# Where q is projected, rotated and multiplied by sin in a one-core attention and mixture-of-experts layer

## The chip, the cores and the metric

The kernel runs on one core of one Trainium2 chip. The metric is device microseconds of one execution. Three executions of the kernel before took 1820.54, 1824.64 and 1824.67 us; their median is 1824.64 us. A further execution was recorded by the hardware profiler, and everything said of engines and waits comes from that one.

A core has five engines, each with its own instruction stream that it works through in order, held together by semaphores. The profile's names for them are PE (TensorE: matrix products, with PEld its weight loads), DVE (VectorE), ACT (ScalarE), POOL (GpSimd) and SP (SyncE, which here only issues DMAs).

## The reference

The layer is causal attention with rotary position codes (16 heads of 64, four sequences of 1024 tokens, width 256), a residual and layer norm, then a mixture of experts (top 3 of 16) with another residual and layer norm. The part that matters here is the head of the attention:

```python
def _rope(x, sin, cos):
    d = x.shape[-1] // 2
    x_hi, x_lo = (x[..., :d], x[..., d:])
    y_lo = x_lo * cos + x_hi * sin
    y_hi = x_hi * cos - x_lo * sin
    return jnp.concatenate([y_lo, y_hi], axis=-1)
proj = x @ W_in.T + b_in
...
q = _rope(q, sin, cos)
k = _rope(k, sin, cos)
att = jnp.einsum('bhqd,bhkd->bhqk', q, k) * jnp.asarray(scale, x.dtype)
att = jnp.where(mask[None, None], att, jnp.asarray(-jnp.inf, x.dtype))
att = jax.nn.softmax(att, axis=-1)
y = jnp.einsum('bhqk,bhkd->bhqd', att, v)
```

All arithmetic is in float32. The kernel keeps q and k transposed, so that the rotation is `q*sin' + swap(q)*cos`, where `swap` exchanges the 32-row halves of each head.

## The kernel before

**Pairs and slots.** The heads are worked through in pairs: 4 sequences times 8 pairs make 32 pairs n = 0 to 31. Each pair has six slots k = 0 to 5, one for each entry of `chunks = [(7,), (6,), (5,), (4,), (3, 2), (1, 0)]`, which are blocks of 128 queries; block 7 has the longest row (1024 keys), block 0 the shortest. The later half of q (queries 512 to 1023, called q1 below) is used in slots 0 to 3, the earlier half (q0) in slots 4 and 5.

**What one slot does.** `scores` (L299) multiplies q by k on PE into four PSUM buffers; DVE passes over each (L307), which adds the mask, copies to `p` and finds the row minimum `nmax`; ACT takes the exponential (L322) with a row sum; DVE inverts the sum (`rinv`, L336); POOL multiplies `p` by it (`divide`, L339); two slots later DVE transposes `p` (`turn`, L356), and PE multiplies it with v (`product`, L377). Beside that, each pair writes a part of the output projection (`out`, L399, summed into `acc` by DVE, L457), computes v for later pairs (`values`, L253, to a DRAM tile `v_d` and back by `spread` as `vr`), and prepares q and k of the next pair.

**Preparing q and k.** `project(n, i, g)` does the matrix product of x with `wqk[n]` (L215, a PSUM tile `pp`); ACT adds the bias and writes `rawq` or `rawk` (L220); DVE multiplies the same `pp` by sin into `rotq` or `rotk` (L221); SP issues four DMAs (L233) that swap the halves into `swq` or `swk`. `rotate` then multiplies the swapped copy by cos (L239) and adds it (L244), on POOL. In the instruction stream the sin product on DVE waits for a count of ACT's that includes the bias instruction on the same `pp`. While pair n runs, the next pair's k is projected in slots 0 and 1 and rotated in slot 2; q1 is projected in slot 2 and rotated in slot 4; q0 is projected in slot 5 and rotated in slot 0 of its own pair.

**PSUM.** The scores, `pp`, `oo` (of `out`) and `vv` (of `values`) all take their tiles in turn from one pool of four buffers (tag `s`). A tile that is the fourth after another takes that one's buffer, and PE waits until its readers are done.

**What sets the order.** PE runs the order of the program text, by `tc.manual_schedule`. The other engines are ordered by a scheduler from the program order and from the edges that `after` adds: in the kernel before, the sin product of every pair but the first is set behind `order["inverse"]`, the slot's `rinv`, and so behind the slot's transposes. POOL's rotations are set behind `order["divide"]`. SP issues its DMAs in the order in which the program makes them, each when what it waits for is there; `wqk` of pair n+2 is loaded by `load_qk` in slot 5 of pair n, and first used by the projection of k in slot 0 of pair n+1.

**The router.** Behind the pairs of each of the first three sequences, `router.batch` picks experts for its tokens: transposes and small DVE operations in pairs 9 to 11 (and 17 to 19, 25 to 27), then 24 `scatter` calls (L681), each an indirect DMA that POOL issues, which write table entries in pairs 12 to 14 (20 to 22, 28 to 30): four each in slots 1 and 3. `residual` (L177) adds the output bias on POOL, in slots 0 and 4 of the last pair of a sequence and near the start. After the last pair the mixture of experts runs, in lines that the change does not touch.

Of the kernel before, what the change touches and what calls it, by code (L numbers as in the profile page):

```python
# [88 lines left out]
def attention(  # L89
# [5 lines left out]
    with ExitStack() as ctx:  # L95
# [41 lines left out]
        def load_v(n):  # L137
            wv[n] = wp.tile([P, DC, 2 * P], FP, tag="wv", name="wv")
            return nc.sync.dma_start(out=wv[n], in_=w_v[n % NP // 2])

        def load_o(n):
            wo[n] = wop.tile([P, D], FP, tag="wo", name="wo")
            return nc.sync.dma_start(out=wo[n], in_=w_outT[ts(n % NP, P)])
# [24 lines left out]
        def load_router():  # L168
            router.start(late)
            for d in (x_b, *sums):  # L170
                late(nc.sync.dma_start(
                    out=d[NT:].rearrange("(p h) d -> p (h d)", p=P), in_=zero
                ))
# [21 lines left out]
        rot = {}  # L195
        raws, swps = {}, {}

        def project(n, i, g):


            b, p = divmod(n, NP)
            if i == 0:
                half = rot[n, 0, g] = qkp.tile([P, 512], FP, tag=f"rotq{g}", name="rotq")
                part = raw = qkp.tile([P, 512], FP, tag="rawq", name="rawq")
                whole = True
            else:
                whole = (n, 1) in rot
                if not whole:
                    rot[n, 1] = qkp.tile([P, T], FP, tag="rotk", name="rotk")
                    raws[n] = qkp.tile([P, T], FP, tag="rawk", name="rawk", bufs=1)  # L210
                half, raw = rot[n, 1][:, ts(g, 512)], raws[n]
                part = raw[:, ts(g, 512)]
            ps = ps_s.tile([P, 512], FP, tag="s", name="pp")
            for c in range(DC):
                nc.tensor.matmul(  # L215
                    ps, lhsT=wqk[n][:, c, i, :], rhs=xts[b, g][:, c, :],
                    start=(c == 0), stop=(c == DC - 1),
                )
            bias = bqk[:, i, p : p + 1]
            nc.scalar.activation(part, ps, AF.Identity, bias=bias)  # L220
            m = nc.vector.scalar_tensor_tensor(  # L221
                half, ps, bias, sin[:, ts(g, 512)], ALU.add, ALU.mult
            )
            if n:
                after(m, "inverse")
            if whole:

                if i == 0:
                    swp = swps[n, 0, g] = qkp.tile([P, 512], FP, tag="swq", name="swq")
                else:  # L230
                    swp = swps[n, 1] = qkp.tile([P, T], FP, tag="swk", name="swk", bufs=1)
                for r in range(4):
                    nc.sync.dma_start(out=swp[ts(r, 32), :], in_=raw[ts(r ^ 1, 32), :])  # L233
# [93 lines left out]
        order = {}  # L327

        def after(i, kind):
            tc.add_manual_dep(i.ins, order[kind].ins.name, NO_SYNC, reason="issue order")  # L330
            return i
# [53 lines left out]
        def close(n):  # L385
            p = n % NP
            yT = yp.tile([P, TC, 4, 32], FP, tag="yT")
            for a, y in enumerate(st.pop(n)):

                nc.scalar.activation(  # L390
                    yT[:, :, a, :], y[:, : 2 * P].rearrange("p (i q) -> p i q", q=32),
                    AF.Identity, bias=bv[:, p : p + 1],
                )
            st[n] = yT.rearrange("p i a q -> p (i a q)")
# [25 lines left out]
        plan = {}  # L420
        first = []

        def one_of(n):
            return 0 <= n < n_pairs

        with tc.manual_schedule(engines={mybir.EngineType.PE}):
            for n in range(n_pairs + 2):
                b, p = divmod(n, NP)
                if n == 2:
                    load_router()  # L430
                for k in range(n_slots):
                    here, before = one_of(n), one_of(n - 1)
                    part, ends = None, []
                    if k == 2 and before:
                        product(n - 1, 1)
                    if here:
                        ends = scores(n, chunks[k])
                    if k < 3 and before:
                        product(n - 1, (4, 2, 0)[k])
                        if k == 2:  # L440
                            close(n - 1)
                    if k >= 3 and here:
                        product(n, 10 - k)
                    if k in (0, 3, 4, 5) and one_of(n - 1 - (k == 0)):
                        part = out(n - 1 - (k == 0), (k - 3) % 4 if k else 3)

                    m, kk = divmod(n * n_slots + k - 2, n_slots)
                    rows = [(qc, h) for h in (1, 0) for qc in chunks[kk] if qc >= 4 * h]
                    last = "scores"
                    for i, (qc, h) in enumerate(rows):  # L450
                        if one_of(m):
                            for hh in range(2):
                                turn(m, qc, hh, h, last)
                                last = "turn"
                        if i == 0 and part:
                            a, ps = part
                            order["sum"] = after(nc.vector.tensor_tensor(a, ps, a, ALU.add), last)  # L457
                            last = "sum"
                    divide(n, ends, last)

                    if k == 0 and one_of(n + 2) and n % 2 == 0:
                        late(load_v(n + 2))
                    if k == 1 and one_of(n):
                        late(load_o(n))
                        spread(n, 1)
                    if k == 4 and one_of(n):
                        spread(n, 0)
                    if k == 5 and one_of(n + 2):
                        late(load_qk(n + 2))

                    if one_of(n + 1):
                        if k in (0, 1, 2, 5):
                            project(n + 1, int(k < 2), int(k in (1, 2)))
                        if k == 2:
                            rotate(n + 1, 1)
                        elif k == 4:
                            rotate(n + 1, 0, 1)
                    if k == 0 and one_of(n):
                        rotate(n, 0, 0)
                    if k == 0 and before:  # L480
                        product(n - 1, 3)
                    m = n + 2 - n % 2
                    if k in (3, 4) and one_of(m):
                        values(m, 2 * (n % 2) + k - 3)
                    if k in (1, 2) and n == 0:
                        values(0, k - 1)
                    if k in (0, 4):
                        if n < 2 and k == 4 * (1 - n):
                            residual(0, n)
                        if p == NP - 1 and b + 1 < B:  # L490
                            residual(b + 1, k // 4)
                    for go in plan.pop((n, k), []):
                        go()
                    if k == 1 and p == 1 and 0 < b < B:
                        normalise(b - 1, sp)
                        steps, place, scatters = router.batch(
                            b - 1, accs[b - 1], ps_s, "s", ps_s, "s"
                        )
                        for i, go in enumerate(steps):
                            plan[n + i // 2, (3, 5, 1, 3)[i]] = [go]  # L500
                        plan[n + 2, 3] = [place]
                        for i in range(6):
                            plan[n + 3 + i // 2, 1 + i % 2 * 2] = scatters[4 * i : 4 * i + 4]
                        if b == B - 1:
                            plan[n + 6, 1] = [lambda: first.extend(router.first_list())]
                            plan[n + 6, 3] = [
                                lambda: first[1](router.on_dve), lambda: first[2](ps_s, "s")
                            ]
                if b + 1 < B:
                    if p == 3:  # L510
                        load_acc(b + 1)
                    if p == 4:
                        late(load_x(b + 1, 0))
                    if p == 6:
                        late(load_x(b + 1, 1))
            assert not plan
# [597 lines left out]
```

## Time and profile before

| | |
|---|---|
| runs, median of three | 1824.64 us |
| the profiled execution: its time | 1823.27 us |
| its span (first to last instruction) | 1821.4 us |
| pairs 0 to 31: first score product to the start of pair 31's | 21.9 to 1291.2 us |
| PE busy, share of the span | 1623.9 us, 89% |
| DVE busy | 1174.7 us, 64% |
| POOL busy | 1096.9 us, 60% |
| ACT busy | 707.4 us, 39% |

The profile is read as follows. In the list of waits a row names who waited, for whom, and the total in us, the times and the longest. In a timeline each row has a start and a length in us, the engine, the line, the operation, what it writes and reads, how many were merged, and in brackets the idle time of the engine before it and what ended it. A row "SPq" is a DMA being issued, not its transfer. The granted clock of PE is a share of full speed: it was 0.95 over the whole execution, and it is either 1.00 or 0.50 in a short stretch.

### The profile page before, as it was taken

The numbers are of one execution on the slowest core, as the hardware profiler recorded it, in microseconds if no ns is written. First come the engines' busy times: TensorE is split into PE (matmuls) and PEld (weight loads), VectorE is DVE, ScalarE is ACT, GpSimd is POOL, SyncE is SP. The second block draws the span as 40 slices with busy tenths as digits, with TensorE's granted clock in tenths as the row PEclk, the third lists the DMA queues.
The fourth block names the chain that finished last, engine by engine and source line by source line (L and its number), as shares of the span: only waits on it lengthen the run. The fifth ranks groups of instructions, "written<-read, shape, count | busy, mean of one in ns | idle before, by whom it ended". The sixth has DMA issues, their size and how long they took to land.

```text
span 1821.4 us, 51884 instructions
## 1 busy us (share of the span) xinstructions
PE 1623.9 (89%) x20920; PEld 1116.8 (61%) x20920; DVE 1174.7 (64%) x3520; ACT 707.4 (39%) x1634; POOL 1096.9 (60%) x1046
## 2 busy tenths in 40 slices
PE   7899999989889998988999998899789999999980
PEld 4555555556555555655555555555468888888870
DVE  5677787787877768788777888777755222222224
ACT  3444444444444434534444443344322222222223
POOL 3655556544476754546775544477666678888542
PEclk9899999899899989999999998899999999999995
DMA  6465544474355445534454463344567989999847
GB/s 181 102 159 137 128 109 106 104 202 109 87 137 125 111 102 142 150 87 125 114 122 120 118 189 89 87 105 102 145 218 181 212 230 245 248 245 241 214 91 277
DMA packets 118167, 272.96 MB, mean 150 GB/s; under 512 B 21874, under 2 KB 72434, under 8 KB 102563
## 3 DMA queue, kind: packets, MB, share of 16 engines
q1 hardware_dynamic: 93122, 239.91, 47.7%
q0 software_dynamic: 24656, 29.68, 9.0%
q8 instruction: 167, 2.74, 0.7%
q14 instruction: 78, 0.63, 0.1%
q10 hardware_dynamic: 144, 0.01, 0.0%
HBM read 183.17 MB, written 52.79 MB: 130 GB/s over the span
## 4 chain that ended last, share of the span: by engine, by line
PE 59%; POOL 10%; DVE 9%; DMA 8%; ACT 7%; issue 6%; SPq 2%; ACTq 0%; POOLq 0%; DVEq 0%
PE s L299 11%; PE ps L882 11%; PE ps L898 10%; PE y_ps L377 10%; PE pp L215 6%; PE oo L399 4%; PE vv L253 4%; DMA wqk<-in_w_qk_dram 4%; POOL p L339 3%; ACT p L322 3%; ACT yT L390 2%; DVE p L307 2%; POOL rotq L244 1%; DMA swk<-rawk 1%; POOL swq L239 1%
## 5 line engine op out<-in xcount | busy, mean ns | idle before, releaser
L339 POOL TENSOR_SCALAR p<-p,rinv 128x512 f32<-128x512 f32 (+7 forms) x512 | 374.3, 746 | 514.9 <-DVE rinv L336 500.0
L322 ACT ACTIVATE p<-p,nmax 128x512 f32<-128x512 f32 (+7 forms) x512 | 391.8, 766 | 563.6 <-DVE nmax L307 543.6
L299 PE MATMUL s<-rotk,rotq 64*128 64x512 f32 (+3 forms) x1536 | 342.5, 539 | 107.6 <-POOL rotq L244 69.0
L299 PEld LDWEIGHTS s<-rotk,rotq 64*128 64x128 f32 x1536 | 155.2, 193 | 280.4 <-POOL rotq L244 96.5
L356 DVE STREAM_TRANSPOSE t_first<-p 128x512 f32<-128x512 f32 (+3 forms) x512 | 275.6, 581 | 0.6 <-POOL p L339 0.5
L215 PE MATMUL pp<-xT,wqk 128*128 128x512 f32 x512 | 251.8, 616 | 20.6 <-DVE nmax L307 10.2
L307 DVE CUSTOM_DVE_ANT_0 p<-s,zero 128x512 f32<-128x512 f32 x256 | 166.3, 687 | 111.8 <-PE s L299 111.6
L377 PE MATMUL y_ps<-t_first,vr 32*64 32x160 f32 (+1 forms) x8192 | 218.7, 343 | 4.5 <-DVE t_first L356 2.7
L912 POOL DMA_INDIRECT sums<-y,ids x112 | 178.9, 1598 | 69.0 <-DVE y L908 40.0
L887 ACT ACTIVATE hid<-ps,w 128x256 f32<-128x256 f32 x224 | 94.1, 471 | 314.5 <-issue 252.1
L903 DVE TENSOR_TENSOR y<-ps,w 128x512 f32<-128x512 f32 x56 | 38.7, 692 | 274.7 <-PE ps L898 274.7
L377 PEld LDWEIGHTS y_ps<-t_first,vr 32*64 32x64 f32 x8192 | 162.5, 132 | 86.0 <-DVE t_first L356 35.2
L882 PE MATMUL ps<-xg,w 128*128 128x256 f32 x896 | 204.5, 382 | 3.6 <-DVE xg L872 3.6
L898 PE MATMUL ps<-w,hid 128*128 128x256 f32 x896 | 202.6, 379 | 0.0
L898 PEld LDWEIGHTS ps<-w,hid 128*128 128x128 f32 x896 | 169.8, 190 | 23.0
L882 PEld LDWEIGHTS ps<-xg,w 128*128 128x128 f32 x896 | 167.1, 191 | 24.7 <-DVE xg L872 3.9
L215 PEld LDWEIGHTS pp<-xT,wqk 128*128 128x128 f32 x512 | 92.3, 192 | 115.2 <-issue 66.4
L399 PE MATMUL oo<-wo,yT 128*128 128x256 f32 x512 | 154.8, 428 | 1.9 <-ACT yT L390 1.7
L377 PEld LDWEIGHTS y_ps<-t_last,vr 32*64 32x64 f32 x7424 | 116.5, 137 | 63.3 <-issue 51.1
L377 PE MATMUL y_ps<-t_last,vr 32*64 32x96 f32 (+3 forms) x7424 | 141.9, 259 | 2.8 <-issue 0.8
L253 PE MATMUL vv<-wv,xT 128*128 128x256 f32 x512 | 136.4, 415 | 0.0
L307 DVE CUSTOM_DVE_ANT_0 p<-s,mask,nmax 128x512 f32<-128x512 f32 (+3 forms) x256 | 130.6, 547 | 4.4 <-PE s L299 3.9
(148 smaller groups left out, 1896.1 us busy)
## 6 DMA issues: line engine op xcount, KB each, us to landing
vr<-v_d SPq DMA_DIRECT2D x256, 256.0 KB
w<-in_wall_dram SPq DMA_DIRECT2D x56, 1154.0 KB
swk<-rawk SPq DMA_DIRECT2D x128, 128.0 KB
swq<-rawq SPq DMA_DIRECT2D x256, 64.0 KB
v_d<-v SPq DMA_DIRECT2D x128, 128.0 KB
wqk<-in_w_qk_dram SPq DMA_DIRECT2D x32, 256.0 KB
xT<-in_xT_dram SPq DMA_DIRECT2D x8, 512.0 KB
wv<-in_w_v_dram SPq DMA_DIRECT2D x16, 256.0 KB
```

The source lines that it names most:

```text
L215: nc.tensor.matmul(ps, lhsT=wqk[n][:, c, i, :], rhs=xts[b, g][:, c, :], start=(c == 0), stop=(c == DC - 1),)
L253: nc.tensor.matmul(ps[:, u, :], lhsT=xts[b, cc // 2][:, c, ts(cc % 2 * 2 + u, P)], rhs=wv[n][:, c, :], start=(c == 0), stop=(c == DC - 1),)
L299: nc.tensor.matmul(s[:, :n_k], lhsT=rot[n, 0, qc // 4][ts(hh, KD), ts(qc % 4, P)], rhs=k[ts(hh, KD), ds(k0, n_k)], start=True, stop=True,)
L307: i = nc.vector.tensor_tensor_reduce(out=probs[n, qc, hh][:, ds(k0, n_k)], in0=s[:, :n_k], in1=mask[:, 512 - n_k :] if last else zero[:, : ...
L322: nc.scalar.activation(pr, pr, AF.Exp, bias=m, scale=-1.0, accum_out=rsum[:, hh : hh + 1])
L339: order["divide"] = router.behind = nc.gpsimd.tensor_scalar(pr, pr, rinv[:, hh : hh + 1], 1.0, ALU.mult, ALU.mult)
L356: order["turn"] = router.on_dve = after(nc.vector.transpose(turned[n][h][:, hh, :, ds(i - 4 * h, n_j, step=7 - 4 * h), :], probs[n, i, hh] ...
L377: nc.tensor.matmul(st[n][a][ts(hh, KD), ds(32 * j, 32 * (TC - j))], lhsT=vrs[n, h][ts(a, 32), jh // 2 * 8 + 2 * u + jh % 2, ts(hh, KD)], r ...
L399: nc.tensor.matmul(ps[:, v, :], lhsT=st[n][:, ts(2 * h + v, P)], rhs=wo[n], start=True, stop=True,)
L882: nc.tensor.matmul(ps[:, f - f0, :], lhsT=w[:, ds(c * FF + f * P, P)], rhs=xg[:, c, :], start=(c == 0), stop=(c == DC - 1),)
L898: nc.tensor.matmul(ps[:, h, :], lhsT=hid[:, f, ts(h, P)], rhs=w[:, ds(W2_AT + f * D, D)], start=(f == 0), stop=(f == FC - 1),)
L912: s = behind(nc.gpsimd.indirect_dma_start(out=sums[t % 2], out_offset=bass.IndirectOffsetOnAxis(ap=ids[:, h, i : i + 1], axis=0), in_=y[:, ...
```

## The change

The projections of q move within slots 2 and 5 from the slot's end to just behind `scores`, ahead of the products (and of `out`). The sin product of q is set behind the slot's last score pass (`order["scores"]`) instead of behind `rinv`, and the slot's first transpose is set behind it (`order["part"]`). The projections of k stay where they were. The rotation of q1 moves from slot 4 to slot 3. Table entries, four in each of slots 1 and 3, become two in slot 0, two in slot 1 and four in slot 5.

```diff
-        def project(n, i, g):
+        def project(n, i, g, kind=None):
...
-            if n:
-                after(m, "inverse")
+            if kind:
+                after(m, kind)
+                order["part"] = m
...
-                    here, before = one_of(n), one_of(n - 1)
-                    part, ends = None, []
+                    here, before, ahead = (one_of(n + i) for i in (0, -1, 1))
+                    part, ends, last = None, [], "scores"
...
                     if here:
                         ends = scores(n, chunks[k])
+
+                    if k in (2, 5) and ahead:
+                        project(n + 1, 0, int(k == 2), last)
+                        last = "part"
                     if k < 3 and before:
                         product(n - 1, (4, 2, 0)[k])
...
-                    last = "scores"
                     for i, (qc, h) in enumerate(rows):
...
-                    if one_of(n + 1):
-                        if k in (0, 1, 2, 5):
-                            project(n + 1, int(k < 2), int(k in (1, 2)))
-                        if k == 2:
+                    if ahead:
+                        if k < 2:
+                            project(n + 1, 1, k, "inverse")
+                        elif k == 2:
                             rotate(n + 1, 1)
-                        elif k == 4:
+                        elif k == 3:
                             rotate(n + 1, 0, 1)
...
-                        for i in range(6):
-                            plan[n + 3 + i // 2, 1 + i % 2 * 2] = scatters[4 * i : 4 * i + 4]
+                        for i in range(3):
+                            for slot, c0, c1 in ((0, 0, 2), (1, 2, 4), (5, 4, 8)):
+                                plan[n + 3 + i, slot] = scatters[8 * i + c0 : 8 * i + c1]
```

In the built instruction streams, slot 2 on PE is then: scores, `pp`, product (before: scores, product, `pp`). Slot 5 is: scores, `pp`, product, `oo` (before: scores, product, `oo`, `pp`). On DVE the sin product of q stands between the last score pass and the first transpose of slots 2 and 5. On ACT `rawq` stands in slot 2 ahead of the four `yT` copies (L390), where it stood behind them; in both slots it stays behind the slot's exponentials. On POOL the pair of q1's rotation stands behind the `divide` of block 4 instead of behind those of blocks 3 and 2. On SP the four `swq` DMAs of slot 5 stand ahead of the load of `wqk`, where they stood behind it. The counts of instructions stay the same on every engine.

## The prediction

> **What bounds the kernel now.** First the busy times, then the list of waits: PE is busy 89% of the span, and its idle time is what a new order can win.
>
> ```profile
> PE 1623.9 (89%) x20920; PEld 1116.8 (61%) x20920; DVE 1174.7 (64%) x3520; ACT 707.4 (39%) x1634; POOL 1096.9 (60%) x1046
> ...
> PE s L299 <- POOL rotq L244: 69.0, 28, 6.3
> PE s L299 <- DVE rotq L221: 31.8, 30, 1.1
> PE pp L215 <- DMA wqk<-in_w_qk_dram: 9.5, 8, 5.1
> ```
>
> The first of the waits is q1's rotation, which the first scores of a pair wait for (28 of 32 pairs); the second is the sin product, which holds the PSUM buffer of the fourth score tile of slot 3; the third is k's first projection of a pair (slot 0), which waits for its weights. The change attacks the first two, at most 101 us. Next the timelines of PE and SP in pair 6, a plain one (slots begin at 249.15, 256.92, 263.73, 269.04, 275.38 and 280.78 us; pair 7 at 286.52).
>
> ```profile
> 244.06 1.07 SPq L263 DMA_DIRECT2D v_d<-v  x2
> 245.17 0.48 SPq L135 DMA_DIRECT2D wqk<-in_w_qk_dram  x1
> 248.98 2.46 SPq L233 DMA_DIRECT2D swq<-rawq  x4
> 249.15 1.99 PE L299 MATMUL s<-rotk,rotq 64*128 64x512 f32 x8 [0.95 <-POOL rotq L244]
> 253.74 1.95 PE L215 MATMUL pp<-xT,wqk 128*128 128x512 f32 x4 [0.41 <-DMA wqk<-in_w_qk_dram]
> ...
> 266.69 0.94 ACT L322 ACTIVATE p<-p,nmax 128x768 f32<-128x768 f32 x1 [3.87 <-DVE nmax L307]
> ...
> 268.15 1.26 DVE L356 STREAM_TRANSPOSE t_first<-p 128x512 f32<-128x512 f32 x2
> 270.70 0.75 DVE L221 SCALAR_TENSOR_TENSOR rotq<-pp,bqk,sin 128x512 f32<-128x512 f32 x1 [1.25 <-ACT rawq L220]
> 271.51 0.49 PE L299 MATMUL s<-rotk,rotq 64*128 64x128 f32 x2 [1.12 <-DVE rotq L221]
> ```
>
> The reader is to see two things. The sin product starts when ACT's `rawq` is done (L220: 269.98 + 0.69), so it is ACT that times it. And `wqk`, issued at 245.17, is waited for until 253.74: 8.6 us for 256 KB.
>
> **Slots 2 and 3.** The sin product now stands ahead of the transposes and still waits for `rawq`, which waits behind two exponentials. In slot 2 of pair 6: exponentials 266.69 to 268.55, `rawq` to 269.24 (`pp` on PE starts when the first score pass frees its buffer, about 265.6, and ends about 267.6, so it is no limit), sin to 269.95. DVE, done with the score passes at 266.92, sits idle 2.3 us where before it transposed at once. Then the transposes (1.23 + 1.20) and `rinv` (0.12): 272.45, against 271.37 for the first score pass of slot 3 before. The 1.12 us stall at the fourth score tile goes: scores run 269.4 to 271.1. But what is late next is `oo` of slot 3, whose buffer is that of slot 3's first score tile: first pass 272.45 + 0.61 + 0.08 = 273.15, where before `oo` ran at 272.60. `oo` and `vv` (0.96 + 1.82) then end at 275.95 against 275.38: **0.57 us lost** in each of 31 pairs, **+17.7 us**. Bounds: -0.55 (if `oo` need not wait, 271.95 + 2.78 = 274.7) to +1.1 (the whole delay of DVE).
>
> **Slot 5 to slot 0.** Without the rotation, PE would go on at once. Scores, `pp`, product and `oo` of slot 5 are 4.88 us by the rows of pair 6 (0.86 + 1.90 + 1.15 + 0.97) against a slot of 5.81; q1's rotation, 2.5 us on POOL, moves into the 3.75 us that POOL idles ahead of its block-3 divides (row at 281.42). DVE's wait for `rawq` in slot 5 (exponentials to 284.7, sin 285.4 to 286.1, all shifted by 0.57) frees the buffers of slot 0's third and fourth tiles in time. But the projection of k in slot 0 comes 4.0 us behind its scores (1.91 + 1.14 + 0.96), so 8.9 us from slot 5's start, and needs `wqk`. Counted from slot 5's start, pairs 2 to 7 began that projection at 10.20, 10.70, 10.06, 10.60, 10.40 and 10.37, five of the six held by the transfer: it is the bound already, and the 0.9 us of waiting for the rotation lay mostly beside it.
>
> **The load behind the swaps.** The change puts the four `swq` issues of slot 5 ahead of `wqk` on SP. They wait for `rawq`, 285.4, and take 2.46 us to issue: `wqk` goes out at 287.9, 6.5 us into slot 5 instead of 1.83. The trace's completion marks show the order of landing. For pair 3 (slot 5 at 130.2): the second `v_d` at 140.1; twelve of `wqk`'s sixteen marks by 136.4 and the last four at 139.7 to 140.7; `swq` at 140.9, 141.1, 141.3, 141.5. So a few of the DMA engines carry `v_d` to its end before they come to what was issued later, and `swq` ends 0.8 us behind `wqk` (0.75 to 1.05 in pairs 2 to 7). With the two swapped I take `wqk` to land where `swq` landed, 10.9 to 11.4, mean 11.0, and the projection at 11.15: **+0.75** against the mean of 10.39. Lower bound: nothing queued, 2.6 us after issue as `wv`'s data took behind `swq` in most pairs, 9.1 us: -1.3. Upper: +1.3, if the later `v_d` backlog adds as in pair 15 (12.06). I stay by the marks, since they are the same rings, only reordered.
>
> Pair by pair, with that landing: pairs 2 to 7 +4.4; 9, 14, 15, 17, 22, 23, 25 +4.2; 10, 18, 26 +0.2; 29 and 30 nothing. Where the rotation was much later, it wins. Pairs 8, 16, 24 had `residual` (2.36 us) between its halves and a 3.2 us gap:
>
> ```profile
> 325.84 2.35 POOL L177 TENSOR_TENSOR acc<-acc,bo 128x1024 f32<-128x1024 f32 x1
> 329.46 3.79 PE L299 MATMUL s<-rotk,rotq 64*128 64x512 f32 x8 [3.23 <-POOL rotq L244]
> 460.25 4.16 PE L299 MATMUL s<-rotk,rotq 64*128 64x512 f32 x8 [5.26 <-POOL rotq L244]
> ```
>
> Their projection was at 14.8 and comes to 10.7: -12.3 for the three. Pairs 11, 19, 27 (5.26 us) are held by the router's DVE work, too: DVE ends its score passes at 457.3, waits for `rawq` until 458.75, and slot 1 comes at 468.0 instead of 469.95: -6.2. Pairs 12 and 20 (3.6 us) for the same reason only -2.4; 13 and 21 -1.8; pair 1 (6.3 us) -3.2; pair 31, which projects nothing behind it, its whole 5.2. Sum **-31.1 and +8.8 = -22.3 us**.
>
> **The table entries.** An issue takes POOL 0.97 + 0.30 us (24 per batch, 31 us). In slot 5 four (5.1 us) fill the 5.1 us that POOL waits ahead of the block-7 divide; in slots 0 and 1 two (2.6 us) stand before waits of 1.9 and 5.0 us. Nothing, while those waits last; without them up to 0.7 us in nine pairs. What they win, earlier rotations in pairs 13 to 15, 21 to 23, 29 to 31, is counted above. The moved rotation does not come too early for its swap: that is issued from 269.3 on in pair 6 and landing takes some 3 us, and POOL reaches it behind the block-4 divide, at about 280.7.
>
> **The granted clock.** New idle time of 2 us or more at slot 0 can halve it.
>
> ```profile
> 540.30:543.70 3.40, 1.38 (x7) 0.53 (x8) 1.47 (x5) 0.69 (x1) 3.32 (x5) 1.00 0.47 94
> 543.70:547.10 3.40, 3.40 (x70) 1.87 (x66) 2.85 (x9) 0.66 (x1) 0.55 (x2) 0.50 0.73 209
> 618.80:622.20 3.40, 1.61 (x7) 0.54 (x7) 1.96 (x5) 0.69 (x1) 3.32 (x5) 1.00 0.50 102
> 622.20:625.60 3.40, 3.40 (x74) 1.83 (x70) 2.97 (x9) 0.88 (x1) 0.82 (x3) 1.00 0.69 187
> ```
>
> The columns are the stretch, its length, busy time of PE, PEld, DVE, ACT and POOL, the clock, then DMA. PE idle for 2.02 us of a 3.4 us stretch is followed by one at 0.50; 1.79 us is not. Some 15 pairs will wait 2.0 us or more (11.15 - 8.9 = 2.2); about half fall wholly into one such stretch; each costs half of 3.4 us: 15 x 0.5 x 1.7 = **+13 us** (bounds 0 and 25 x 1.7 = 43). What the present gaps cost by the clock is in the pair times above. [...]
>
> **Sum.** 17.7 - 22.3 + 13 = +8.4 us on the profiled 1823.3 (span 1821.4, 1.9 around it): 1831.7; the median stands 1.4 higher: **1833 us**.
>
> **Rivals.** (a) *The waits go and nothing takes their place.* If `wqk` lands when it did, the slot-0 losses (+8.8) go, the gains rise by about 4, no clock is lost: 17.7 - 35 = -17; with `wqk` unqueued at 9.1, each of some 25 pairs wins 1.3 more: about -46. 1779 to 1808. For it: 69 us stand in one row and SP is idle then. Against: the eight waits for `wqk`, in pairs where the rotation was late, too. (b) *Gain and loss cancel*: the sum without the clock, -4.6 us, or with a few halvings: 1819 to 1830. For it: 1.75 us gaps (pairs 23, 30) left the clock alone. (c) *The late load bites harder*: 0.5 us more in each of 25 pairs and a halving in most: 8.4 + 12.5 + 25: 1870. It decides from a landing of 11.5 on. (d) The change not doing what it says: in a plain pair the rotation ends near 283 on POOL, well before PE can use it near 286, so it leaves the path; only its price is open.
>
> **How the numbers follow.** A measurement tells 0.3% (5.5 us) from no change. The forecast, slower by 6 to 35 us (1830 to 1860), has 0.48; (c) beyond it 0.06; (b) 0.17; (a) 0.29. So faster 0.29, same 0.17, slower 0.54. The forecast's own range is 1830 to 1860; the one that leaves out a tenth at either end is 1796 to 1862.
>
> **What would show it.** Right: the wait of L299 for POOL `rotq` nearly gone; that for DVE `rotq`, too; the wait of `pp` (L215) for `wqk` grown from 9.5 to 40 us or more; `oo` (L399) waiting for DVE some 30 times by about 1 us; DVE idle before `rotq` for ACT over 80 us (47.2 now); more stretches at 0.50 in slot 0. Wrong: `wqk` landing below 10 us from slot 5, or slots 2 and 3 together no longer than now.

## The result and the profile after

17 executions of the changed kernel took 1819.22 us (median; 1807.98 to 1832.09), 17 of the kernel before beside them 1823.42 us (1812.13 to 1831.40). The ratio is 0.9994, 95% interval 0.9974 to 1.0014: no change that can be measured. Two further measurements, made beside the experiments below, gave 0.9994 (0.9970 to 1.0018) and 1.0030 (1.0008 to 1.0052).

The profiled execution of the changed kernel took 1814.91 us, span 1813.1 us, 8.3 us less than that of the kernel before. Its list of waits (who waited, for whom; us in total, times, longest):

```profile
DVE rotq L221 <- ACT rawq L220: 120.5, 60, 2.2
...
PE oo L400 <- DVE nmax L308: 39.8, 33, 1.6
PE pp L215 <- DMA wqk<-in_w_qk_dram: 34.2, 20, 5.3
PE pp L215 <- DVE nmax L308: 21.5, 34, 3.6
PE pp L215 <- DVE acc L461: 10.0, 6, 2.0
...
PE s L300 <- POOL rotq L245: 5.4, 2, 3.2
```

The 69.0 us for the rotation are down to 5.4, and the 31.8 us for the sin product are gone. In their place stand 39.8 us of `oo`, 34.2 us for `wqk` (9.5 before) and, in six router pairs, 10 us for DVE's sum: the projection of slot 5 now comes ahead of the products and takes the PSUM buffer of slot 4's `oo` sooner. DVE's wait for `rawq` rose from 47.2 to 120.5 us; its row in the kernel before:

```profile
DVE rotq L221 <- ACT rawq L220: 47.2, 50, 1.3
```

The timelines of pair 6 (slots at 251.4, 260.3, 267.07, 272.81, 279.23 and 284.62 us, pair 7 at 289.43) show it one by one:

```profile
270.26 0.08 DVE L308 DVE_READ_ACCUMULATOR2_ANT nmax<- 128x1 f32 x1
...
271.89 0.67 ACT L220 ACTIVATE rawq<-pp,bqk 128x512 f32<-128x512 f32 x1
...
272.59 0.75 DVE L221 SCALAR_TENSOR_TENSOR rotq<-pp,bqk,sin 128x512 f32<-128x512 f32 x1 [2.24 <-ACT rawq L220]
...
275.71 0.66 DVE L308 CUSTOM_DVE_ANT_0 p<-s,zero 128x512 f32<-128x512 f32 x1
...
276.44 1.13 PE L400 MATMUL oo<-wo,yT 128*128 128x256 f32 x4 [1.17 <-DVE nmax L308]
...
288.62 3.02 SPq L234 DMA_DIRECT2D swq<-rawq  x4
291.69 0.58 SPq L135 DMA_DIRECT2D wqk<-in_w_qk_dram  x1
...
295.17 1.95 PE L215 MATMUL pp<-xT,wqk 128*128 128x512 f32 x4 [1.46 <-DMA wqk<-in_w_qk_dram]
```

DVE stands 2.24 us for `rawq`; its next score pass begins at 275.71, and `oo` waits for it 1.17 us. In the kernel before, `oo` of that slot ran without a wait of its own:

```profile
272.60 1.13 PE L399 MATMUL oo<-wo,yT 128*128 128x256 f32 x4
```

In the changed kernel `wqk` goes out 7.1 us into slot 5 and PE waits for it until 295.17, which is 10.55 us into slot 5.

The next table is worked out from the traces: for pairs 1 to 30, the time from the first score product of a slot to that of the next, summed, in us. "Clock" is half of the time that these pairs spent at a granted clock of 0.50. It is what the halving could cost at most: part of it falls on idle time, and in the changed kernel a 128x256 matmul of `oo` took 634 ns (median) in the stretch at 0.50 from 439.02 us, against 379 at 1.00 in pair 6. The two later profiles of the changed kernel are from the chips C and A of the next section; rotation alone, the old entries and slot 2's sin are from C, the other variants from A.

```
                                    slot 0     1      2      3      4      5      sum   clock
before                               249.6  221.7  163.5  219.8  161.6  216.6  1232.8   54.9
changed                              279.3  230.0  172.2  209.9  171.4  165.2  1228.0   25.6
changed, the two later profiles      280.1  231.2  172.2  216.7  171.4  166.6  1238.2   41.0
                                     278.1  230.6  172.2  215.0  173.2  169.1  1238.2   44.4
rotation alone                       293.7  221.2  161.2  215.2  163.1  161.9  1216.4   47.8
rotation and table entries           278.5  228.8  162.3  217.9  161.2  159.9  1208.7   44.4
changed, old table entries           310.9  222.0  173.0  222.7  170.5  169.9  1269.0   61.4
changed, early load                  233.1  232.1  172.2  226.5  170.9  165.2  1200.0   34.1
changed, early load, slot 2's sin    229.8  234.1  173.5  208.5  160.9  172.8  1179.5   35.1
before, early load                   242.2  224.3  162.8  223.4  162.7  215.0  1230.3   60.5
```

From the first line to the second: slot 5 gave 51.4 us and slot 3 gave 9.9 us, while slot 0 took back 29.7, slots 2 and 4 took 18.5, slot 1 took 8.3. The profile of the changed kernel was also a good draw of its clock: the two later ones lost up to 41 and 44 us to it, not 26, and have pair sums 5 us above the kernel before.

### The profile page after: what moved, and what is told of

The parts are those of the page before. It is cut to its first block, busy times and chain, and to the rows that moved or that the text cites. A ratio compares the mean times of both kernels' runs of the same rounds, so it can differ in the third digit from the quotient of the medians.

```text
span 1813.1 us, 51966 instructions
## 1 busy us (share of the span) xinstructions
PE 1610.2 (89%) x20920; PEld 1096.3 (60%) x20920; DVE 1174.3 (65%) x3520; ACT 708.4 (39%) x1634; POOL 1099.8 (61%) x1046
## 4 chain that ended last, share of the span: by engine, by line
PE 44%; DVE 18%; issue 9%; POOL 9%; DMA 8%; ACT 7%; SPq 4%; ACTq 0%; POOLq 0%; DVEq 0%
PE ps L887 11%; PE ps L903 10%; PE y_ps L378 6%; PE pp L215 5%; PE s L300 5%; ACT p L323 4%; POOL p L340 4%; SPq L234 4%; DVE t_first L357 3%; DVE t_last L357 3%; DMA wqk<-in_w_qk_dram 3%; PE vv L254 3%; DMA swk<-rawk 2%; PE oo L400 2%; DVE p L308 2%
## 5 line engine op out<-in xcount | busy, mean ns | idle before, releaser
L300 PE MATMUL s<-rotk,rotq 64*128 64x512 f32 (+3 forms) x1536 | 324.2, 516 | 12.6 <-POOL rotq L245 5.4
L215 PE MATMUL pp<-xT,wqk 128*128 128x512 f32 x512 | 264.1, 641 | 73.3 <-DMA wqk<-in_w_qk_dram 34.2
L300 PEld LDWEIGHTS s<-rotk,rotq 64*128 64x128 f32 x1536 | 147.4, 187 | 157.0 <-issue 73.9
L400 PE MATMUL oo<-wo,yT 128*128 128x256 f32 x512 | 147.5, 412 | 41.4 <-DVE nmax L308 39.8
L254 PE MATMUL vv<-wv,xT 128*128 128x256 f32 x512 | 129.0, 398 | 5.4 <-DVE nmax L308 5.4
```

The lines of the kernel that those rows point to most:

```text
L215: nc.tensor.matmul(ps, lhsT=wqk[n][:, c, i, :], rhs=xts[b, g][:, c, :], start=(c == 0), stop=(c == DC - 1),)
L254: nc.tensor.matmul(ps[:, u, :], lhsT=xts[b, cc // 2][:, c, ts(cc % 2 * 2 + u, P)], rhs=wv[n][:, c, :], start=(c == 0), stop=(c == DC - 1),)
L300: nc.tensor.matmul(s[:, :n_k], lhsT=rot[n, 0, qc // 4][ts(hh, KD), ts(qc % 4, P)], rhs=k[ts(hh, KD), ds(k0, n_k)], start=True, stop=True,)
L400: nc.tensor.matmul(ps[:, v, :], lhsT=st[n][:, ts(2 * h + v, P)], rhs=wo[n], start=True, stop=True,)
```

## The experiments

Each stands beside runs of the kernel before on its own chip. Five groups were run, on chips called A, B, C, D and again A here; the kernel before took 1819 (A), 1900 (B), 1825 (C), 1906 (D) and 1819 us (A). On B and D something else is slow (last section), so that a number from these two is only set beside others of the same group.

### Where the load of `wqk` stands

**The load ahead of the swaps again (A).** On SP only, the order of slot 5 is put back:

```diff
+                    if k == 5 and one_of(n + 2):
+                        late(load_qk(n + 2))
                     if k in (2, 5) and ahead:
                         project(n + 1, 0, int(k == 2), last)
...
-                    if k == 5 and one_of(n + 2):
-                        late(load_qk(n + 2))
```

> The changed kernel with one thing undone: on SP the load of wqk stands ahead of slot 5's four swq issues again, as before the change. Theory A (the v_d backlog holds the load, not its place on SP): wqk lands at most 0.5 us sooner than the 10.4 us from the start of slot 5 that the changed kernel showed; the wait of pp (L215) for wqk goes from 34.2 us to 22-34, the time by 0 to -8 us. Rival B (its place on SP decides, as the prediction had it: the two change places): wqk lands some 0.8 us sooner, about 9.6, the wait falls below 15 us, and the time by 12 to 20 us.

Measured: 1806.97 us, 0.9934 (0.9907 to 0.9961), 12.5 us under the kernel before. Both theories had half of it. The landing moved as A said: in pairs 2 to 8 `wqk` landed 10.25 us into slot 5 instead of 10.71 (10.19 in the kernel before), so the `v_d` backlog is taken to be the larger part of it. The time fell about as B said: slot 0 lost 11.5 us over pairs 1 to 30. The row of the wait (30.0 us) hides this, since some waits for the same transfer are put down to DVE.

**The load in slot 2 (A).**

```diff
-                    if k == 5 and one_of(n + 2):
+                    if k == 2 and one_of(n + 2):
                         late(load_qk(n + 2))
```

> The changed kernel with the load of wqk three slots sooner, in slot 2 behind the swq issues. Theory A (with the rotation out of the way, the load is what slot 0 waits for): the wait of 34.2 us for wqk is gone, the projection of k in slot 0 starts 8.9-9.3 us from slot 5's start instead of 10.5, some 20 pairs win 1.2-1.5 us: 25-35 us less than the changed kernel, ratio to before 0.980-0.987. Rival B (another wait takes its place: the fourth PSUM buffer, DVE's score passes, which stand at 21.5 us now): that row grows to 40 us or more and the time falls by under 10 us.

Measured: 1785.59 us, 0.9805 (0.9778 to 0.9832). Theory A holds: of the wait for `wqk` one of 5.6 us is left, at the start, and slot 0 fell from 279 to 233 us. That is 46 us in slot 0, of which slot 3 took back 17 (209.9 to 226.5; 10 and 12 against the two later profiles of the changed kernel). Nothing in slot 3 had been changed. The stretches of its profile (its length, busy time of PE, PEld, DVE, ACT, POOL, the clock, DMA) show how, in pairs 6 and 7:

```profile
266.85:270.26 3.41, 2.24 (x49) 1.49 (x47) 3.41 (x9) 1.45 (x4) 0.52 (x1) 1.00 0.34 85
270.26:273.67 3.41, 3.41 (x8) 2.78 (x9) 3.35 (x11) 1.74 (x4) 3.41 (x3) 0.50 0.18 68
304.39:307.81 3.42, 2.85 (x68) 1.77 (x49) 3.25 (x7) 1.70 (x5) 0.00 (x0) 1.00 0.28 71
307.81:311.22 3.41, 2.81 (x14) 2.22 (x14) 3.41 (x12) 1.73 (x4) 3.30 (x3) 1.00 0.34 88
```

Both pairs have the same 1.17 us stall ahead of `oo`. In pair 6 it falls whole into one stretch of the clock, and the next one is granted 0.50; in pair 7 it falls across a border and costs nothing more. Pair 6 took 38.17 us, pair 7 36.56.

**The same early load in the kernel before (A).** The same edit.

> The kernel before with nothing changed but the load of wqk three slots sooner, in slot 2. Theory A (before the change the rotation and the load lay side by side ahead of slot 0's projection, so that taking one away leaves the other): the 9.5 us of waiting for wqk go, the 69 us for the rotation stay, and the time falls by 5 to 12 us; ratio 0.993-0.997. Rival B (the load was the bound in most plain pairs): 20 us or more less, ratio under 0.989.

Measured: 1820.43 us, 1.0003 (0.9983 to 1.0022): neither. The rotation's 69 us stayed (68.9), as A said; slot 0 won 7.4 us, and slots 1 and 3 gave 6.2 back, with 5.6 us more of halved clock.

### Where the sin product stands

**Behind `rinv` again (A).** `project` issues the product and `rawq` at once, and the rest later:

```diff
+            def finish():
...
+                if n:
+                    after(m, "inverse")
...
-                        project(n + 1, 0, int(k == 2), last)
-                        last = "part"
+                        finish = project(n + 1, 0, int(k == 2), last)
...
                     divide(n, ends, last)
+                    if k in (2, 5) and ahead:
+                        finish()
```

> The changed kernel with the sin product of q set back behind rinv, and so behind the slot's transposes, on DVE; the projection stays just behind the scores on PE, rawq where the change put it on ACT, the rotation in slot 3 and the table entries where they are. Theory A (the sin product ahead of the transposes costs DVE an idle 2.3 us, and oo of slot 3 waits for it): the wait of oo (L400) for DVE nmax goes from 39.8 us to under 8, DVE's wait for ACT rawq from 120.5 to under 50; slots 2 and 3 together shorten by 0.5 to 1.1 us in each of 31 pairs: 15 to 35 us less than the changed kernel, ratio to before 0.981-0.992. Rival B (the sin product then holds the fourth score tile's buffer again, as in the kernel before): a wait for DVE rotq of 25 us or more comes back and the time stays within 5 us of the changed kernel.

Measured: 1817.94 us, 0.9986 (0.9961 to 1.0011). Rival B holds. The wait of `oo` is gone, and the waits of PE begin with

```profile
PE s L304 <- DVE rotq L223: 51.7, 57, 1.0
```

in most pairs twice, for the PSUM buffer that the sin product holds: at the fourth score tile of slot 3 and at the scores of slot 0. The stall changes its name.

**Only slot 2's sin product behind `rinv`, with the early load (B, then C).** As above with `k == 2`; in slot 5 the sin product stays ahead of the transposes.

> The changed kernel with the load of wqk in slot 2 (as in the run that had that alone, 0.9805) and, in slot 2 only, the sin product set back behind the transposes and rinv; in slot 5 it stays ahead of them. Theory A (slot 3's stall, wherever it lies, is what halves the clock there: with the sin product behind rinv slot 3 took 6.18 us instead of 6.42 and it was seldom halved): slot 3 at 6.2 us, some 10 halved stretches fewer in the pairs than the 26 of that run, 20 to 35 us less than it, ratio to before 0.961-0.970. Rival B (the stall only changes its name, from oo to the fourth score tile, and the halvings stay): 0 to 8 us less, ratio 0.976-0.981.

> The changed kernel with the load of wqk in slot 2 and slot 2's sin product behind rinv, once more. About 1820 for the kernel before: theory A 0.961-0.972 (below the 0.9805 of the early load alone); rival B 0.976-0.983 (the stall in slot 3, now for the fourth score tile, halves the clock as often as the stall ahead of oo did). About 1900: 0.961-0.970, as measured there.

Measured: 0.9657 (0.9614 to 0.9699) on B, and on C 1769.70 us, 0.9703 (0.9664 to 0.9743): 55 us less than the kernel before, the fastest version of all, and within theory A's range on both. Against the early load alone (a profile from A), slot 3 fell from 226.5 to 208.5 us and slot 4 from 170.9 to 160.9. But the reason given was only half right: the clock's loss left slot 3 (27.1 to 15.4 us) and came back above all in slot 5 (0 to 10.2); its sum is unchanged (34.1 and 35.1). What was won is unhalved time.

### The rotation, the table entries and the rest, one by one

First on chip B:

> The kernel before with one part of the change alone: q1 is rotated in slot 3 instead of slot 4. Theory A (the rotation is a real bound only where it is much later than the load of wqk): the wait of L299 for POOL rotq falls from 69 to under 10 us, that of pp for wqk grows from 9.5 to 20-30, plain pairs 2 to 7 change by under 0.3 us each at full clock, and the gains in pairs 8/16/24, 11/19/27, 12/20 and 31 leave 15 to 30 us: ratio 0.984-0.992. Rival B (POOL's rotation in slot 3 delays the divides behind it, and PE waits for those): ratio 0.997 or more, and a new row of 20 us or more of PE or DVE waiting for POOL.

> The changed kernel with the rotation back in slot 4 and the table entries back in slots 1 and 3, so the move of the projection and of the sin product alone. Theory A (this part is pure loss: 0.5 us in slots 2 and 3 of 31 pairs, the load of wqk behind the swq issues): the wait for oo (L400) stays at 35-42 us, the wait for POOL rotq at 50 us or more, time 8 to 25 us above before: ratio 1.004-1.014. Rival B (slot 5, shorter by the sin product off its end, gives it back): ratio 0.998-1.002.

> The changed kernel with the table entries back in slots 1 and 3. Theory A (they cost nothing in either place but for nine pairs): ratio to before within 0.004 of the changed kernel's 0.9994, and only pairs 12 to 14, 20 to 22, 28 to 30 differ. Rival B (in slot 3 they hold up q1's rotation on POOL, which now stands there): the wait for POOL rotq grows from 5.4 to 15 us or more, time 8 to 20 us more, ratio 1.004-1.010.

The edits are the change's own lines, taken over or put back; for the rotation:

```diff
-                        elif k == 4:
+                        elif k == 3:
                             rotate(n + 1, 0, 1)
```

Measured: rotation alone 0.9873 (0.9830 to 0.9916), as A said. Projection and sin product alone 0.9964 (0.9935 to 0.9993): neither; slot 2 of a plain pair is 5.74 us and slot 3 6.42, the loss foreseen, but the whole is not slower there. Changed kernel with the old entries 0.9851 (0.9796 to 0.9906): neither. On this chip the profile of the rotation alone has the first of these rows; the second is that of the kernel before, which has no profile from B:

```profile
PE y_ps L377 <- issue: 34.4, 68, 1.8
PE y_ps L377 <- issue: 2.2, 6, 1.3
```

So all of it was set beside the changed kernel on another chip (C):

> The changed kernel itself, so that the parts can be set beside it on one chip: the last four runs fell on another chip than all runs before them, on which the kernel before took 1900 us, and the pairs behind table entries (12 to 14, 20 to 22, 28 to 30) stood 5 to 12 us longer each, with PE waiting for nothing the profile shows (rows 'issue' ahead of L378). If the kernel before takes about 1820 here: ratio 0.997-1.002. If it takes about 1900: theory A (what is slow there is whatever runs beside the table entries, and the change moves these to slots 0, 1 and 5): ratio 0.975-0.985, and under the run with the old table entries (0.9851).

> The kernel before with q1 rotated in slot 3 alone, once more. On a chip where the kernel before takes about 1820, theory A: 0.984-0.992, so that this part alone is faster than the whole change; rival B: 0.997 or more. About 1900: within 0.983-0.992, as measured there.

> The changed kernel with the table entries back in slots 1 and 3, once more. On a chip where the kernel before takes about 1820, theory A (the entries' place costs nothing there): within 0.003 of the changed kernel in this call. About 1900, theory A (the entries hold up PE there): 0.003 to 0.012 above the changed kernel in this call. Rival B, in both: the entries' place decides the whole result, 0.01 or more either way.

Measured, with the kernel before at 1824.62 us: the changed kernel 1824.15, 0.9994; the rotation alone 1797.89, 0.9850 (0.9811 to 0.9889); the changed kernel with the old table entries 1853.40, 1.0157 (1.0114 to 1.0199). Theory A holds for the rotation. For the entries rival B holds: moving eight DMA issues a pair (in nine pairs) is worth 29.3 us here, and without it the change would be 1.6% slower. They do not act by holding up POOL, as the rival of the run on B had it: PE's wait for POOL `rotq` is 4.4 us with the old places and 5.4 with the new. The profile with the old entries, pair 13 to 14 (slot 5 from 584.40 us, pair 14 from 589.42):

```profile
583.61 1.05 POOL L685 DMA_INDIRECT table<-pair,slots  x1 [0.17 <-issue]
...
585.12 1.07 SPq L264 DMA_DIRECT2D v_d<-v  x2
...
586.14 0.99 POOL L685 DMA_INDIRECT table<-pair,slots  x1 [0.17 <-issue]
...
588.70 0.97 POOL L685 DMA_INDIRECT table<-pair,slots  x1 [0.30 <-issue]
...
590.91 0.58 SPq L135 DMA_DIRECT2D wqk<-in_w_qk_dram  x1
...
597.35 3.75 PE L215 MATMUL pp<-xT,wqk 128*128 128x512 f32 x4 [3.75 <-DMA wqk<-in_w_qk_dram]
```

and the changed kernel at the same place (slot 5 from 583.38, pair 14 from 588.18):

```profile
589.89 0.58 SPq L135 DMA_DIRECT2D wqk<-in_w_qk_dram  x1
...
592.29 1.06 POOL L686 DMA_INDIRECT table<-pair,slots  x1 [0.16 <-issue]
...
594.30 1.95 PE L215 MATMUL pp<-xT,wqk 128*128 128x512 f32 x4 [1.84 <-DVE t_first L357]
```

With the old places the entries are issued while `v_d` is on its way, ahead of `wqk`; with the new ones behind both. POOL's own time for them is the same. The last row's wait is put down to a transpose, but PE starts 0.14 us after `wqk` lands (10.79 us into slot 5). The completion marks of the transfers, counted from the start of slot 5, mean us:

```
                              pairs 2 to 8              pairs 13-15, 21-23, 29, 30
                          2nd v_d   wqk  projection      2nd v_d   wqk  projection
before                       9.36  10.19   11.01            9.88  10.70   11.36
rotation alone               9.36  10.20   10.34           10.93  11.82   11.95
rotation and entries         9.34  10.18   10.32            9.80  10.53   10.67
changed, old entries         8.86  10.50   10.64           11.20  12.92   13.06
changed (on C)               8.83  10.56   10.70            8.88  10.63   10.76
```

In the eight pairs behind table entries `v_d` lands later with the old places, 2.3 us in the changed kernel and 1.1 beside the rotation alone, and `wqk` behind it. In the changed kernel with the old places PE waits 2.6 to 5.1 us in these pairs, and the clock is halved in their slot 0, mostly for two stretches: of the 37 us that they lose, up to 26 are halved clock (34.1 against 8.5).

Then, on chip D, with what was open:

> The kernel before with the rotation in slot 3 and the table entries in slots 0, 1 and 5: the change without the move of the projection and of the sin product. Theory A (the projection's move is the part that costs, 17.7 us in slots 2 and 3 and some 10 at slot 0 and in the clock, the entries win little where the load still goes out at 1.8 us into slot 5): the waits of 1.3 to 4 us for wqk in pairs 13, 15, 22, 23, 29 and 30 fall under 1.5; 5 to 15 us less than the rotation alone (0.985): ratio 0.976-0.983 on a chip where before takes about 1820. Rival B (the entries' move gives its 29 us here too): 0.966-0.972, and the projection's move costs the 56 us whole.

> The changed kernel with the table entries back in slots 1 and 3 and the load of wqk in slot 2. Theory A (the entries cost only through the transfer that slot 0 waits for: in slot 3 their writes lie ahead of v_d and wqk): the waits of 2.6 to 5.1 us in pairs 13 to 15, 21 to 23, 29 and 30 are gone and the time is that of the early load with the new places, ratio 0.977-0.985. Rival B (they slow something else in those pairs): those pairs stay 3 us or more longer than pairs 2 to 7, ratio 0.992 or more.

> The kernel before with the table entries in slots 0, 1 and 5 alone. Theory A (slot 0's projection waited beside the late rotation there, so an earlier wqk in nine pairs shows little): -2 to -10 us, ratio 0.994-0.999. Rival B: the move gives 20 us or more by itself, ratio under 0.99. Rival C (nothing, as the prediction had it): 0.999-1.002.

> The kernel before with the rotation in slot 3, the table entries in slots 0, 1 and 5 and the load of wqk in slot 2; projection and sin product where they were before. Theory A (the first two parts and an early load without the part that costs): plain pairs 36.5 us, some wait of 1.1 us for the fourth score tile in slot 3; ratio 0.962-0.972, near the 0.9703 of the changed kernel with the early load and slot 2's sin product behind rinv. Rival B (the halvings in slot 3 grow as the pairs get shorter and eat the gain, as in the kernel before with the early load): 0.975 or more.

Measured: rotation and entries 0.9787 (0.9732 to 0.9841); changed kernel with old entries and early load 0.9727 (0.9678 to 0.9776); entries alone 0.9944 (0.9908 to 0.9980); rotation, entries and early load 0.9836 (0.9788 to 0.9884). The first lies in theory A's range, which was meant for a chip on which the kernel before takes about 1820 us, and the third too, at its edge. The second answers how the entries act: with the load out of their way, no wait for `wqk` is left in any of those pairs. So they act through the transfer. The ratio lies below theory A's range. Three of the eight pairs (13, 14, 22) still took 40.6 to 42.3 us, where most plain ones took 36.5 to 38.2: the excess lies in slots 2 and 5, where PE stalls on D (last section), so that rival B is not excluded there. The fourth missed: on this chip the early load gained nothing without the projection's move, and the loss to halved clock in pairs 0 to 30 rose from 57.6 to 81.6 us, as rival B had it.

Last, on A again:

> Rotation in slot 3 and table entries in slots 0, 1 and 5, without the move of the projection and the sin product. On a chip where the kernel before takes about 1820: theory A (the projection's move costs some 0.5 us in slots 2 and 3, 0.4 at slot 0 and some clock in 31 pairs, about 30 us): ratio 0.974-0.984, so 0.015-0.025 below the changed kernel; rival B (it costs the 56 us that the runs with the old entries show): 0.966-0.972. About 1900: 0.973-0.984 as before, and theory A 0.008-0.025 below the changed kernel, rival B 0.03 or more below it.

> The changed kernel beside it. On a chip where the kernel before takes about 1820: 0.997-1.002 as in both runs so far. About 1900: theory A (there the slots behind the table entries stall PE, and the change moves the entries to slots 0, 1 and 5): 0.985-1.000; rival B: under 0.98.

Measured: 1786.39 us, 0.9817 (0.9786 to 0.9848), and 1822.99 us, 1.0030 (1.0008 to 1.0052), just above what was expected. Theory A holds in the sum: the move of the projection and the sin product costs 36.6 us, with the entries in their new place; and the rotation and the entries without it are 1.8% faster than the kernel before. The table above says where, for 29.5 of the 36.6 us, since the profiled execution without the move was the slowest of its five: slot 2 takes 9.9 us more and slot 3 2.9 less; slot 4 takes 12.0 and slot 5 9.2 more (up to 9.3 of both is halved clock), above all in the six router pairs (10, 11, 18, 19, 26, 27), where DVE is late. Slot 0, for which theory A had 0.4 us a pair, takes nothing more in all (-0.4).

## Why the prediction was wrong, step by step

It forecast 1833 us, slower by half a per cent, in a range of 1796 to 1862, and the result is no change: its rival (b), cancelling, came true. Its sum was -31 and +39, and a remainder of +8 stands close to the 5.5 us that can be measured at all. The next table sets its terms beside the traces: the change in us against the trace of before, from the first scores of pair 0 to those of pair 31, in the three profiled executions of the changed kernel. In brackets stands how much of it is halved clock, at most.

```
                                    forecast   first profile        C              A
a slot 5 and the slot 0 behind it     -9.3     -25.9 (-23.9)  -23.7 (-18.8)  -23.2 (-13.6)
slots 2 and 3                        +17.7      +0.7 (-13.7)   +7.5  (-6.8)   +5.7  (-8.5)
slots 1 and 4                          0       +18.3  (+6.8)  +19.3 (+10.2)  +20.8 (+10.2)
all, with slot 0 of pair 0            +8.4      -8.2 (-32.3)   +3.1 (-15.4)   +1.9 (-13.4)
```

The -9.3 is -31.1 + 8.8 + 13. Each line misses by 10 us or more, and the misses nearly cancel: that the forecast change, +8.4, is only 4 to 13 us from the three measured ones (-4.2, -0.5, +4.4) is in part luck.

- **The clock, +13 us at slot 0.** This is the step that failed. Without it the sum is -4.6 us, which is no change. Some 15 pairs were to wait 2.0 us or more; 5 or 6 did, since the projection began at 10.7 to 10.85 us instead of 11.15. In the pairs where the wait for `wqk` is new or longer (2 to 7, 9, 12, 14, 15, 17, 20, 22, 23, 25, 29, 30), halvings cost at most 3.4 to 6.8 us more than before. At the same time halvings went: what those of slot 0 cost in pairs 1 to 30 fell from 27.2 us to between 8.5 and 11.9. The prediction had the cost of the old ones in its pair times, and its -22.3 without the 13 is close to the -23 to -26 of the table. But it counted no clock at slot 3, where 0.50 followed a stall of 1.17 us (shown above) and whose loss fell from 23.9 us to between 10.2 and 17.1. Over all slots of pairs 1 to 30 the clock lost 10.5 to 29.3 us less than before, where 13 more was forecast.
- **Slots 2 and 3, +17.7 us.** The mechanism held step by step: DVE stood 2.24 us (2.3 foreseen), `oo` waited 1.17 us. In a plain pair the two slots are 12.16 us against 11.66, +0.50 for +0.57 foreseen. Over all pairs that is 14 us, of which fewer halvings gave back 7 to 14.
- **Slots 1 and 4, put at nothing.** They took 18 to 21 us. In slot 4 (9.7 to 11.6 us) it is the six router pairs: PE waits 1.4 to 1.6 us for DVE's score passes, and in slot 5 the projection, in its earlier place, another 1.3 to 2.0 us for DVE's sum (rows below). Slot 1 (8.6 to 9.5 us) grows with the entries in their new places (221.2 to 228.8 us beside the rotation alone); up to 5.1 to 8.5 us of it is halved clock in the changed kernel. Why is open.
- **The rotation, -31.1 us.** Alone it gives -26.7 us (0.9850, C). Right in kind and nearly in size.
- **The table entries, "Nothing, while those waits last".** This reasoning failed too. It counted POOL's time for issuing them and the order on POOL, not the writes they issue. Beside the whole change their move is worth 29.3 us (C). Beside the rotation alone it took the ratio from 0.9850 to 0.9817 (C and A): some 6 us, with intervals of 6 to 7 us to either side of each, so not told from nothing. The forecast was spared by luck: it took one landing of `wqk`, 11.0, for all pairs, and in the eight pairs behind table entries that is near only with the new places (10.6; 12.9 with the old). The trace of before had a sign of it: `wqk` landed at 12.06 in pair 15, which the prediction used as an upper bound "if the later `v_d` backlog adds as in pair 15" without asking what was different in that pair.
- **The load behind the swaps, +8.8 us.** Its place on SP costs some 11 us (0.9934 against 0.9994). Right in size. The landing was 10.5 to 10.7 instead of 11.0: it did not take the place of `swq`; the second `v_d` came 0.5 us sooner.
- **Smaller sums.** Three of the prediction's sums do not follow from its rows: pairs 9 to 25 give +3.5, not +4.2; pairs 8, 16 and 24 come to 10.7 where its own landing gives 11.15 (-11.0, not -12.3); rival (a)'s lower end is -50, not -46. Together they change the forecast by under 1 us.

The waits in slots 4 and 5 of a router pair, pair 11 of the changed kernel (slot 4 from 487.61 us):

```profile
492.13 1.13 PE L400 MATMUL oo<-wo,yT 128*128 128x256 f32 x4 [1.62 <-DVE nmax L308]
...
498.50 1.98 PE L215 MATMUL pp<-xT,wqk 128*128 128x512 f32 x4 [2.04 <-DVE acc L461]
```

The parts as measured, -27 for the rotation, -6 for the entries and +37 for the rest, add up to +4; the whole was measured at -0.5 to +4.4 us in those two groups. The +37 is near the forecast +39, but made up otherwise: slot 0 gave 0.4 us where 21.8 were to be lost, slots 2 and 3 took 7.0 instead of 17.7, slots 4 and 5 took 21.2 instead of nothing. Of what would show it, the waits for the rotation, the sin product, `oo` and `rawq` came as written (5.4, gone, 33 times, 120.5); the wait for `wqk` was 34 us, not 40; the stretches at 0.50 in slot 0 became fewer, not more.

## What to carry to other kernels

A DMA issue for which its engine has time can still hold up other transfers (here `wqk` landed at 12.9 instead of 10.6 us): ask what is waiting for a transfer at that moment, and cost it by the pairs in the trace where the two already meet. When a long wait is removed, the second in line is known (here the load of `wqk`): moving it too took the ratio to 0.9805. The same edit gained nothing in the kernel before (1.0003), where the first wait still stood. Where the clock halves behind stalls (here behind one of 1.17 us in slot 3), count the halvings that go with the old stalls, in every slot, as well as those that come with new ones. A forecast that is the small difference of two large sums is a forecast of no change.

## What the hardware showed beside this

**What stood ahead of the halvings.** Idle time alone does not tell. In the kernel before, a stretch of 3.41 us with 1.07 us of idle PE (from 564.17 us, in slot 3 of pair 13) was followed by 0.50, and one with 1.96 us (from 717.77 us, in slot 1 of pair 17) was not. In the changed kernel 16 stretches at 1.00 in pairs 1 to 30 have the stall of slot 3, 1.16 or 1.17 us, as their idle time. Seven of them were followed by 0.50, and these have all 40 matmuls of slot 3's `product` (`32*64 32x32`) in them; the other nine have 1 to 34 of them. What in a stretch decides is not shown by these counts, and no run was made on it.

**Chips B and D.** The kernel before took 1900 us on B and 1906 on D, 4 to 5% more than the 1819 and 1825 on A and C. On B and D PE stood still ahead of `product` with nothing to wait for in the slots behind table entries. The row of this wait has 34.4 us for the rotation alone on B (above) and 26.5 for the old entries with the early load on D, against 3.1 for the changed kernel on C and 5.1 for rotation and entries on A. The pairs show it: in the run of the rotation alone, pairs 13 and 14 took 45.0 and 44.8 us, pair 15 36.5. On C the same kernel took 41.4, 37.4 and 41.4 us. The cause is open; no run was made on it. Open is also why the projection's move is no loss on B: not alone (0.9964), and not beside the rotation with the old entries (0.9851 against 0.9873 without it), where C shows 1.0157 against 0.9850. The changed kernel itself was not run on B or D, so the result and the prices above are those of A and C.
